# Moving element-wise work between engines in a scan kernel: residuals on VectorE, five products of twelve on GpSimd, and a PSUM bank counted as free later

## The chip, the cores and the metric

The kernel runs on one core of a Trainium2 chip. The core has five engines, each with its own in-order queue of instructions: TensorE (PE, matrix products into PSUM), VectorE (DVE), ScalarE (ACT), GpSimd (POOL) and SyncE (SP), which here only issues DMAs. They wait for one another through semaphores. SBUF is the working memory with 128 partitions; PSUM has eight banks of 128 x 512 float32 numbers, and all eight are used. The metric is the device time of one execution in microseconds, taken as the median of several runs; lower is better.

## The reference

The input is x of shape (4, 96, 64, 64), four images of 96 channels and L = 4096 pixels. Four layers follow one another.

- Layer 0 normalises by groups, multiplies up to 192 channels, applies a 3 x 3 depthwise convolution and SiLU, and then scans the pixels in four orders (rows, columns, and both backwards). The scan is the heart of it: for each of 4 directions, 192 channels and 16 states,

```python
dA = jnp.exp(dt_[..., None] * A[None])
hst = hst * dA + (dt_ * ut)[..., None] * bt[:, :, None, :]
y = jnp.einsum('bkdn,bkn->bkd', hst, ct)
```

 where dt comes out of a softplus, and bt and ct (B and C below) are per state and pixel, shared by the channels. The four directions are summed, normalised over the channels and multiplied down to 96; x is added.
- Layer 1 is an inverted bottleneck: 96 to 576 channels, ReLU, a 3 x 3 depthwise convolution, ReLU, back to 96; x is added.
- Layer 2 normalises each token, mixes the tokens through a 4096-point FFT with a ReLU between transform and inverse, adds the result to x, and then adds a feed-forward network: h = relu(q(q(xn) W1 + b1)), y = q(h W2 + b2), with inputs and weights rounded to an 8-bit and sums to a 16-bit float.
- Layer 3 adds attention without a softmax, which reduces to a product of small matrices per image, plus a bias, and then a feed-forward network like that of layer 2.

## The kernel before

**The scan in units.** A step is one chunk of 512 pixels of one direction of one image: 4 images x 4 directions x 8 chunks = 128 steps. A step has 12 units: 64 channels by 8 states, laid out as 128 partitions by two halves of 512. For each unit,

- GpSimd multiplies the input term with B (`inputs`, line 1206, tile db, 128 x 1024),
- ScalarE forms the two decays exp(A dt) in two PSUM banks of the tag "da" (`decays`, L1216), of which there are four, so two units' worth,
- VectorE runs the two scans (`states`, L1225),
- the states are multiplied with C. There are two kinds of unit. Where the unit's number in its step is in POOL_C, the scans write SBUF (tile hc), GpSimd multiplies both halves in one instruction (`product`, L1244) and copies the final state (L1241). In the others the scans write back into the da banks, VectorE multiplies each half with C into hc (L1229) and ScalarE copies the two final states (L1239). Before, POOL_C holds six of the twelve units,
- TensorE sums the states of two units into the bank "y" (`sums`, L1265), three portions after the first of them, and ScalarE evicts it (L1276).

**The order by portions.** The loop over `slot` in `scans` writes one portion per unit, and the order of the instructions in it is the order of each engine's queue: the DMAs that are due, the decays of the next unit, the product of the last one, db of the unit after the next, the scans of this unit, the sums that are due, and then side work. The side work is everything else: the front of later images (layer 0's convolution and softplus inputs), layers 1 to 3 of earlier images. It is written as generators that yield the engine and the rough cost of the next instruction (`yield ac(0.65)` for ScalarE, `dv` for VectorE, `pe` for TensorE with the number of banks it takes); `advance` takes a step of some stream if the engine has room in this portion (`SHARE`) and if a bank is free. The side work has three banks of the tag "mm", and `held_banks` counts them: `bank` adds one, `free` takes one off. Ahead of each portion's side work the loop also takes `freed[0]` off, which nothing fills before the change.

**Softplus.** `scan_inputs` computes, for each third of the channels, a matmul (L594, L598) into a bank p, three activations on ScalarE (L603, L605, L607), a maximum and sum on VectorE (L609), a product on VectorE (L612), and a copy on ScalarE (L616) that reads p last; then `free()`.

**The feed-forward network.** `feed_forward` normalises (`layer_norm`, L858 to L872), and for each third of the hidden units multiplies (L884), rounds to 16 bits while evicting (L887), adds the bias and applies the ReLU, and rounds to 8 bits. The ReLU is on VectorE (L892) where `alone` is set, and on ScalarE (L895) elsewhere. After the second product (L905) follow the rounding (L908) and the bias (L911) on ScalarE, and the residual: two matmuls with an identity (L914 for the 16-bit result, L915 for x) and a copy on ScalarE (L917). `layer_2` and `layer_3` add their first residual in the same manner, with a matmul of x with the identity (L1030, L1086) into the same bank and an eviction with the bias (L1032, L1088).

**After the scans.** When the loop is over, the list `alone` is filled and the rest is written outside the portions: what is left of layer 1 and all of layers 2 and 3 of the last image, three chunks of 512 pixels at a time. In this part the banks of the scans are taken in turn too.

Of the kernel before, what the change touches and what calls it, by code (L numbers as in the profile page):

```python
# [22 lines left out]
AF = mybir.ActivationFunctionType  # L23
ALU = mybir.AluOpType
# [3 lines left out]
B, C, H, W = 4, 96, 64, 64  # L28
# [13 lines left out]
KORDER = [(0, 1, 3, 2)] * (B - 1) + [(1, 3, 0, 2)]  # L42

SCAN = {"rep_d": 3, "rep_g": 3, "rep_BC": 5, "db": 3, "hc": 5}
POOL_C = (1, 3, 5, 7, 9, 11)
TMP, IN = 10, 5

PC = NI * NJ // 2
# [46 lines left out]
def hybrid_kernel(ctx: ExitStack, tc: tile.TileContext, a: dict):  # L95


    pe, ac, dv = ((lambda us, banks=0, ind=False, e=e: (e, us, banks, ind)) for e in ("pe", "act", "dve"))
    wait = lambda n: ("wait", n, 0, False)
    nc = tc.nc  # L100
    mm = nc.tensor.matmul
    act = nc.scalar.activation
# [11 lines left out]
    alone = []  # L114
# [12 lines left out]

    held_banks, freed = [0], [0]

    def free(n=1):  # L130

        held_banks[0] -= n


    tc.keep_in_program_order(nc.scalar.preload_act_table_set("natural_log_exp_and_others"))
# [5 lines left out]
    def const(name, rows=slice(0, 128)):  # L141
        return cst[rows, CS[name]]

    def col(name, i=0, rows=slice(0, 128)):
        at = COL[name].start + i
        return cols[rows, at : at + 1]
# [29 lines left out]
    def xn_rows(c, rows=128):  # L176
        return xn[:rows, c * RPC : (c + 1) * RPC, :]
# [44 lines left out]
    def chunk(c):  # L222
        return slice(c * CH, (c + 1) * CH)
# [26 lines left out]
    wa2 = small.tile([128, 2, C], F32, name="wa2")  # L250
# [5 lines left out]
    m2 = small.tile([128, C], F32, name="m2")  # L256
    sd, td = (small.tile([128, NT1], F32, name=n) for n in ("sd", "td"))
    t2, ta2 = (small.tile([C, 1], F32, name=n) for n in ("t2", "ta2"))
# [169 lines left out]
    def later(out, t, then=None):  # L428

        to_store.append((out, t, then))  # L430
# [140 lines left out]
    def scan_inputs(b, u, o, c, done):  # L571

        i = b % 3
        if not done.issuperset([c] if o == 0 else range(NCH)):
            while not done.issuperset([c] if o == 0 else range(NCH)):
                yield wait(1)
            yield wait(2)
        ua, ub = u
        yield pe(1.8, 1)
        p = bank()  # L580
        mm(p, lhsT=sel[:, o, 0, :], rhs=view(ua, o, c), start=True, stop=False)
        mm(p, lhsT=sel[:, o, 1, :], rhs=view(ub, o, c), start=False, stop=True)

        yield ac(0.7)
        xd = tmp("xd")
        act(xd, p, AF.Identity, bias=col("one"))
        free()
        for e in (0, 1):
            later(d_bc[o + 2 * e][i][c], xd[64 * e : 64 * e + 2 * NS])
        for part in range(3):  # L590
            yield pe(0.9, 1, part > 0)
            p = bank()
            if part < 2:
                mm(p, lhsT=dtw[:, o + 2 * part, 0:128], rhs=xd, start=True, stop=True)  # L594
                at = [(slice(0, 128), o + 2 * part, slice(0, 128))]
            else:
                for e in (0, 1):
                    mm(p[64 * e : 64 * e + 64], lhsT=dtw[:, o + 2 * e, 128:DI], rhs=xd, start=True, stop=True)  # L598
                at = [(slice(64 * e, 64 * e + 64), o + 2 * e, slice(128, DI)) for e in (0, 1)]

            yield ac(0.65)
            z = tmp("z")
            act(z, p, AF.Abs)  # L603
            yield ac(0.65)
            act(z, z, AF.Exp, scale=-1.0)  # L605
            yield ac(0.65)
            act(z, z, AF.Ln, bias=1.0)  # L607
            yield dv(0.7)
            nc.vector.scalar_tensor_tensor(p, p, 0.0, z, ALU.max, ALU.add)  # L609
            yield dv(0.85)  # L610
            g = tmp("g")
            nc.vector.tensor_mul(split(g), split(p), view(ub if part == 2 else ua, o, c))  # L612
            for rows, k, ch in at:
                later(d_du[k][i][c][ch], g[rows])
            yield ac(0.6)
            nc.scalar.copy(z, p)  # L616
            free()
            for rows, k, ch in at:
                later(d_delta[k][i][c][ch], z[rows])
        traced[b].add((o, c))  # L620
# [254 lines left out]
    def feed_forward(x, weights):  # L875

        wq1, wq2, bq = weights
        xq = tmp("xq", (128, CH), F8)
        yield from layer_norm(x[:C], xq)
        hq = tmp("hq", (128, 3, CH), F8)  # L880
        for m in range(3):
            yield pe(0.5, 1, m > 0)
            p = bank()
            mm(p, lhsT=wq1[:, m * 128 : (m + 1) * 128], rhs=xq, start=True, stop=True)  # L884
            yield ac(0.65)
            acc = tmp("acc16", (128, CH), F16)
            nc.scalar.copy(acc, p)  # L887
            free()
            if alone:

                yield dv(0.75)
                nc.vector.tensor_scalar(acc, acc, bq[:, m : m + 1], 0.0, ALU.add, ALU.max)  # L892
            else:
                yield ac(0.65)
                act(acc, acc, AF.Relu, bias=bq[:, m : m + 1])  # L895
            if alone and m == 1:
                yield dv(0.75)
                nc.vector.tensor_copy(hq[:, m, :], acc, saturate=False)
            else:
                yield ac(0.65)  # L900
                nc.scalar.activation(hq[:, m, :], acc, AF.Copy, saturate=False)  # L901
        yield pe(1.4, 1)
        p = bank()
        for m in range(3):
            mm(p[:C], lhsT=wq2[:, m, :], rhs=hq[:, m, :], start=m == 0, stop=m == 2)  # L905
        yield ac(0.65)
        acc = tmp("acc16", (128, CH), F16)
        nc.scalar.copy(acc[:C], p[:C])  # L908
        free()
        yield ac(0.65)  # L910
        act(acc[:C], acc[:C], AF.Identity, bias=bq[:C, 3:4])  # L911
        yield pe(1.4, 1)
        p = bank()
        mm(p[:C], lhsT=ident16, rhs=acc[:C], start=True, stop=False)  # L914
        mm(p[:C], lhsT=const("ident", slice(0, C))[:, :C], rhs=x[:C], start=False, stop=True)  # L915
        yield ac(0.65)
        nc.scalar.copy(x[:C], p[:C])  # L917
        free()

    def load_x(src, c):  # L920
# [95 lines left out]
    halves_of = {}  # L1016

    def layers_2_and_3(b):
# [3 lines left out]
        def layer_2(c):  # L1022

            x, first = load_x(d_x2[im], c), load_x(d_half[im], c)
            yield wait(3)
            yield pe(2.7, 1)
            p = bank()
            mm(p[:C], lhsT=wa2[:C, 0, :], rhs=first[:C], start=True, stop=False)
            mm(p[:C], lhsT=wa2[:, 1, :], rhs=halves_of[b][:, chunk(c)], start=False, stop=False)
            mm(p[:C], lhsT=const("ident", slice(0, C))[:, :C], rhs=x[:C], start=False, stop=True)  # L1030
            yield ac(0.65)
            act(x[:C], p[:C], AF.Identity, bias=ta2)  # L1032
            free()
            yield from feed_forward(x, ffn[0])
            later(d_x4[im][:C, chunk(c)], x[:C])
            yield from layer_norm(x[:C], xn_rows(c, C), C)
            kv = [tmp("kv"), tmp("kv")]
            for half, t in enumerate(kv):
                yield pe(0.9, 1, half > 0)
                p = bank()  # L1040
                for n in (0, 1):
                    for e in (0, 1):
                        mm(p[64 * e : 64 * e + 64, 2 * C * n : 2 * C * n + 2 * C],
                           lhsT=xn[:, c * RPC + 4 * half + 2 * n + e, :], rhs=wkv, start=True, stop=True)
                yield ac(0.6)
                nc.scalar.copy(t[:, : 4 * C], p[:, : 4 * C])
                free()
            yield pe(0.9, 1)
            pg = bank()
            for n in range(4):  # L1050
                of = kv[n // 2][:, 2 * C * (n % 2) : 2 * C * (n % 2) + 2 * C]
                mm(pg[:C, :C], lhsT=of[:, C:], rhs=of[:, :C], start=n == 0, stop=n == 3)
            yield dv(0.2)
            if "vk" not in small_sums:
                small_sums["vk"] = bp.tile([C, C], F32, name="vk", bufs=1)
                nc.vector.tensor_copy(small_sums["vk"], pg[:C, :C])
            else:
                nc.vector.tensor_add(small_sums["vk"], small_sums["vk"], pg[:C, :C])
            free()
# [20 lines left out]
        def layer_3(c):  # L1080
            x = load_x(d_x4[im], c)
            yield wait(3)
            yield pe(1.8, 1)
            p = bank()
            mm(p[:C], lhsT=m2, rhs=xn_rows(c), start=True, stop=False)
            mm(p[:C], lhsT=const("ident", slice(0, C))[:, :C], rhs=x[:C], start=False, stop=True)  # L1086
            yield ac(0.65)
            act(x[:C], p[:C], AF.Identity, bias=col("bff", rows=slice(0, C)))  # L1088
            free()
            yield from feed_forward(x, ffn[1])  # L1090
            later(a["out"][b][:, chunk(c)], x[:C])

# [480 lines left out]
```

## Time and profile before

| | |
|---|---|
| median of three runs | 6704.47 us (6701.09 to 6705.06) |
| the profiled execution: time, span | 6709.47 us, 6707.7 us |
| VectorE busy in the span | 5391.2 us (80%) |
| GpSimd busy | 5488.7 us (82%) |
| ScalarE busy | 4269.2 us (64%) |
| TensorE busy | 4872.1 us (73%) |
| first scan, last scan | from 79 us to 6208 us |
| products with C on GpSimd (L1244) | 768 x 2361 ns |
| products with C on VectorE (L1229) | 1536 x 692 ns (two to a unit) |

The profile is of one execution. Its page lists groups of instructions by line of the kernel, engine and tiles, with their number, busy time and mean length, and the idle time of the engine just before them with what ended it. A view of the waits sums, for each pair of lines, how long the first waited for the second. A view by windows gives each engine's busy time in a stretch of the span. The chain that ended last is followed back from the last instruction, at each step to what released it. Ends of matmuls are modelled by the profiler. A float32 matmul appears as two instructions.

### The profile page before, as it was taken

The page shows a single profiled execution, that of the slowest core. Times are in us where ns is not written, and L with a number is a line of the kernel's source. Part 1 is how long each engine was busy: PE and PEld are TensorE (multiplying, and loading weights), DVE is VectorE, ACT ScalarE, POOL GpSimd, SP SyncE. Part 2 cuts the span into 40 slices and gives each one's busy share as a digit, 9 for nine tenths or more (in the row PEclk, how much of TensorE's full clock was granted, in tenths as well). Part 3 has the DMA queues.
Part 4 walks back from the last instruction along what each step waited for, and adds up shares of the span by engine and source line. Part 5 has one row for each costly group of instructions (what it writes and reads, how often), then busy time and mean ns, then how long its engine had stood idle before and what let it go on. Part 6 is the DMA issues. An engine that isn't in the chain of part 4 may idle for free. (4 is left out here: it accounts for less than half of the span.)

```text
span 6707.7 us, 84354 instructions
## 1 busy us (share of the span) xinstructions
PE 4872.1 (73%) x27884; PEld 1775.4 (26%) x27884; DVE 5391.2 (80%) x5611; ACT 4269.2 (64%) x8008; POOL 5488.7 (82%) x2983
## 2 busy tenths in 40 slices
PE   7624767656987776775688877777887776859998
PEld 2101212111223521221122254211223521212383
DVE  5979888788989888888899887988988888888021
ACT  5744776654665677877466657866665676756356
POOL 4868778788999999977999988999999899899000
PEclk9756878768998887886799877878998877869998
DMA  5644555566544544455764445465644554554131
GB/s 189 197 150 144 183 189 181 174 218 219 184 148 143 199 158 147 155 186 188 246 214 146 143 160 167 157 219 186 188 147 146 189 161 161 200 180 156 35 94 38
DMA packets 438824, 1121.41 MB, mean 167 GB/s; under 512 B 73002, under 2 KB 74768, under 8 KB 437140
## 3 DMA queue, kind: packets, MB, share of 16 engines
q1 hardware_dynamic: 438388, 1116.02, 50.7%
q8 instruction: 222, 3.64, 0.2%
q14 instruction: 214, 1.75, 0.1%
HBM read 881.28 MB, written 239.01 MB: 167 GB/s over the span
## 5 line engine op out<-in xcount | busy, mean ns | idle before, releaser
L1206 POOL TENSOR_TENSOR db<-rep_g,rep_BC 128x1024 f32<-128x1024 f32 x1536 | 3602.0, 2365 | 194.1 <-DVE ps_da L1225 115.0
L1216 ACT ACTIVATE ps_da<-rep_d,aneg 128x512 f32<-128x512 f32 x3072 | 2053.5, 689 | 499.4 <-DVE hc L1225 381.7
L1225 DVE TENSOR_TENSOR_SCAN ps_da<-ps_da,state,db 128x512 f32<-128x512 f32 x1344 | 1722.9, 1282 | 371.8 <-ACT state L1239 226.7
L1244 POOL TENSOR_TENSOR hc<-hc,rep_BC 128x1024 f32<-128x1024 f32 x768 | 1813.4, 2361 | 131.8 <-DVE hc L1225 64.8
L1225 DVE TENSOR_TENSOR_SCAN hc<-ps_da,state,db 128x512 f32<-128x512 f32 x1344 | 1645.8, 1266 | 173.0 <-ACT ps_da L1216 155.9
L1265 PE MATMUL ps_y<-hc,cst 128*32 128x512 f32 x6144 | 1037.4, 755 | 781.5 <-POOL hc L1244 759.5
L1229 DVE TENSOR_TENSOR hc<-ps_da,rep_BC 128x512 f32<-128x512 f32 x1536 | 1062.3, 692 | 91.3 <-DVE ps_da L1225 1.3
L1265 PEld LDWEIGHTS ps_y<-hc,cst 128*32 128x32 f32 x6144 | 141.7, 119 | 1450.8 <-POOL hc L1244 1096.0
L1241 POOL COPY state<-hc 128x2 f32<-128x2 f32 x672 | 128.4, 191 | 395.3 <-DVE hc L1225 374.1
L1239 ACT COPY state<-ps_da 128x1 f32<-128x1 f32 x1344 | 212.8, 158 | 343.9 <-DVE hc L1229 343.0
L805 PE MATMUL ps_mm<-h,wd 128*32 128x512 f32 x3192 | 365.7, 593 | 7.7 <-ACT r L154 7.0
L543 PE MATMUL ps_mm<-xp,taps 128*128 128x512 f32 x576 | 299.3, 660 | 42.5 <-ACT xp L523 15.7
L1276 ACT COPY yt<-ps_y 128x512 f32<-128x512 f32 x256 | 149.9, 585 | 222.3 <-PE ps_y L1265 212.2
L594 PE MATMUL ps_mm<-xd,dtw 128*128 128x512 f32 x256 | 176.9, 785 | 156.9 <-ACT z L616 131.9
L782 PE MATMUL ps_mm<-wd,w 128*32 128x512 f32 x2128 | 271.4, 624 | 22.9 <-DMA wd<-x 12.8
L1225 DVE TENSOR_TENSOR_SCAN ps_da<-ps_da,db 128x512 f32<-128x512 f32 x192 | 234.6, 1222 | 56.9 <-ACT state L1239 36.0
L1225 DVE TENSOR_TENSOR_SCAN hc<-ps_da,db 128x512 f32<-128x512 f32 x192 | 223.4, 1204 | 17.3 <-ACT ps_da L1216 13.2
L603 ACT ACTIVATE z<-ps_mm 128x512 f32<-128x512 f32 x192 | 114.3, 596 | 189.1 <-PE ps_mm L594 112.4
L609 DVE SCALAR_TENSOR_TENSOR ps_mm<-ps_mm,z 128x512 f32<-128x512 f32 x192 | 131.9, 687 | 84.0 <-ACT z L607 56.4
L864 PE MATMUL ps_mm<-r,cst 128*128 128x512 f32 x210 | 144.9, 778 | 62.7 <-ACT r L154 17.4
L940 PE MATMUL ps_mm<-wa,xp 128*64 128x96 f32 x1728 | 133.3, 317 | 71.0 <-DVE d L944 62.3
L786 ACT ACTIVATE h<-ps_mm 128x512 f32<-128x512 f32 x266 | 153.9, 596 | 44.6 <-PE ps_mm L782 42.5
(418 smaller groups left out, 6879.9 us busy)
## 6 DMA issues: line engine op xcount, KB each, us to landing
rep_BC<-bc SPq DMA_DIRECT2D x512, 512.0 KB
rep_g<-du SPq DMA_DIRECT2D x384, 512.0 KB
rep_d<-delta SPq DMA_DIRECT2D x384, 512.0 KB
y<-yt SPq DMA_DIRECT2D x512, 128.0 KB
du<-g SPq DMA_DIRECT2D x128, 256.0 KB
delta<-z SPq DMA_DIRECT2D x128, 256.0 KB
tab<-in_etab SPq DMA_DIRECT2D x128, 256.0 KB
ypart<-y SPq DMA_DIRECT2D x72, 256.0 KB
```

Of the source, the lines that this page charges most:

```text
L543: mm(p, lhsT=taps[:, t, 0:128], rhs=window(t, c + e), start=t == 0, stop=t == 8)
L594: mm(p, lhsT=dtw[:, o + 2 * part, 0:128], rhs=xd, start=True, stop=True)
L782: mm(p[32 * n : 32 * n + 32], lhsT=w1[:, 32 * g : 32 * g + 32], rhs=xin[:, n : n + 15 : 2, 1 : W + 1], start=True, stop=True)
L786: act(h[:, :, 1 : W + 1], split(p), AF.Relu)
L805: mm(p[32 * n : 32 * n + 32], lhsT=held["wd"][:, groups[i], o, dx, :], rhs=here[i][:, :, dx : dx + W], start=dx == 0, stop=dx == 2)
L1206: nc.gpsimd.tensor_mul(x["db"], x["step"]["g"][x["i"]], both(x["step"]["BC"][x["j"]][:, 0]))
L1216: act(x["da"][e], x["step"]["d"][x["i"]][:, e], AF.Exp, scale=aneg[:, av : av + 1])
L1225: nc.vector.tensor_tensor_scan(x["h"][e][:, order], x["da"][e][:, order], x["db"][:, e, order], start, ALU.mult, ALU.add)
L1229: x["made"] = nc.vector.tensor_mul(x["hc"][:, e], x["h"][e], x["step"]["BC"][x["j"]][:, 1])
L1239: nc.scalar.copy(to[:, e : e + 1], x["h"][e][:, end : end + 1])
L1244: x["made"] = nc.gpsimd.tensor_mul(x["hc"], x["hc"], both(x["step"]["BC"][x["j"]][:, 1]))
L1265: done = mm(y[32 * q : 32 * q + 32], lhsT=const("stack"), rhs=x["hc"][:, e], start=first or (x["pass"] == 0 and x["j"] == 0), stop=last or ...
```

## The change

Four things are edited.

1. `POOL_C` holds five units of twelve instead of six, and other ones: 1, 3, 6, 8 and 10. Seven units of a step are now multiplied on VectorE.
2. In softplus, `free(behind=True)` replaces `free()`: the bank is counted as free only when the side work of the next portion begins, instead of at once.
3. In the tail, where `alone` is set, the residuals are added by VectorE: the first by one `scalar_tensor_tensor` that reads the bank, the bias and x (a new helper `residual`), the second by one `tensor_add` of x and the 16-bit result, so that the matmuls with the identity and the evictions fall away. Inside the scans they stay as they were.
4. The ReLU of the second third of the hidden units (m == 1) is on VectorE inside the scans too.

```diff
-POOL_C = (1, 3, 5, 7, 9, 11)
+POOL_C = (1, 3, 6, 8, 10)
...
-    def free(n=1):
-
-        held_banks[0] -= n
+    def free(behind=False):
+
+        (freed if behind else held_banks)[0] += 1 if behind else -1
...
             nc.scalar.copy(z, p)
-            free()
+            free(behind=True)
...
-            if alone:
+            if alone or m == 1:
...
         act(acc[:C], acc[:C], AF.Identity, bias=bq[:C, 3:4])
+        if alone:
+            yield dv(0.9)
+            nc.vector.tensor_add(x[:C], x[:C], acc[:C])
+            return
         yield pe(1.4, 1)
...
+    def residual(p, x, bias):
+
+        if alone:
+            yield dv(0.75)
+            nc.vector.scalar_tensor_tensor(x[:C], p[:C], bias, x[:C], ALU.add, ALU.add)
+        else:
+            mm(p[:C], lhsT=const("ident", slice(0, C))[:, :C], rhs=x[:C], start=False, stop=True)
+            yield ac(0.65)
+            act(x[:C], p[:C], AF.Identity, bias=bias)
+        free()
...
-            mm(p[:C], lhsT=wa2[:, 1, :], rhs=halves_of[b][:, chunk(c)], start=False, stop=False)
-            mm(p[:C], lhsT=const("ident", slice(0, C))[:, :C], rhs=x[:C], start=False, stop=True)
-            yield ac(0.65)
-            act(x[:C], p[:C], AF.Identity, bias=ta2)
-            free()
+            mm(p[:C], lhsT=wa2[:, 1, :], rhs=halves_of[b][:, chunk(c)], start=False, stop=bool(alone))
+            yield from residual(p, x, ta2)
...
-            mm(p[:C], lhsT=m2, rhs=xn_rows(c), start=True, stop=False)
-            mm(p[:C], lhsT=const("ident", slice(0, C))[:, :C], rhs=x[:C], start=False, stop=True)
-            yield ac(0.65)
-            act(x[:C], p[:C], AF.Identity, bias=col("bff", rows=slice(0, C)))
-            free()
+            mm(p[:C], lhsT=m2, rhs=xn_rows(c), start=True, stop=bool(alone))
+            yield from residual(p, x, col("bff", rows=slice(0, C)))
```

## The prediction, made before the changed kernel was run

> **What bounds the kernel now.** The page's slices show two regimes: the scans (about 79 to 6208 us), in which VectorE and GpSimd are both over 80% busy, and a tail of 500 us in which GpSimd is idle. The page's costliest groups give the prices (engine, operation, tiles, count, busy us, mean ns):
>
> ```profile
> L1244 POOL TENSOR_TENSOR hc<-hc,rep_BC 128x1024 f32<-128x1024 f32 x768 | 1813.4, 2361 | 131.8 <-DVE hc L1225 64.8
> L1229 DVE TENSOR_TENSOR hc<-ps_da,rep_BC 128x512 f32<-128x512 f32 x1536 | 1062.3, 692 | 91.3 <-DVE ps_da L1225 1.3
> ```
>
> One product on GpSimd is 2.36 us, the same on VectorE 2 x 0.69. Next I cut the span by stages (busy us of PE, PE's loads, VectorE, ScalarE, GpSimd; clock, DMA share, GB/s): a front, a convolution, layers 2 and 3 inside the scans, the tail.
>
> ```profile
> 599.00:1046.00 447.00, 294.49 (x884) 82.05 (x884) 377.83 (x401) 298.73 (x551) 348.45 (x189) 0.78 0.55 178
> 1630.00:2103.00 473.00, 392.94 (x2275) 109.83 (x2272) 430.49 (x437) 299.96 (x587) 466.10 (x256) 0.93 0.52 169
> 2382.00:2781.00 399.00, 262.65 (x937) 75.58 (x934) 352.07 (x360) 320.75 (x622) 385.42 (x212) 0.78 0.45 149
> 6208.00:6708.00 500.00, 439.23 (x4022) 251.01 (x4014) 77.42 (x155) 263.83 (x413) 2.37 (x1) 0.94 0.18 56
> ```
>
> The convolution holds 131 of the db products, 11 steps of 12 units: 43.0 us a step, GpSimd 99% busy. Layers 2 and 3: 9 steps of 44.3 us, GpSimd 97%, VectorE 88%. The front: 8 steps of 55.9 us, GpSimd 78%, VectorE 85%. Who keeps VectorE waiting, in the convolution and then in the layers (total us, times, longest):
>
> ```profile
> DVE ps_da L1225 <- POOL db L1206: 29.1, 42, 1.1
> DVE ps_da L1225 <- ACT state L1239: 5.0, 4, 2.5
> ```
> ```profile
> DVE ps_da L1225 <- ACT state L1239: 18.2, 19, 2.4
> DVE hc L1225 <- ACT ps_da L1216: 8.2, 11, 1.5
> ```
>
> In the convolution GpSimd alone ends VectorE's waits; in the layers it is ScalarE, itself late behind side matmuls. In the whole kernel's waits softplus shows: TensorE waits for the copy that frees a bank, then ScalarE for that matmul.
>
> ```profile
> PE ps_mm L594 <- ACT z L616: 131.9, 59, 6.2
> ACT z L603 <- PE ps_mm L594: 112.4, 70, 5.1
> ```
>
> In the tail the chain that ended last runs through the residuals (start us, us, what):
>
> ```profile
> 6535.66 0.63 ACT acc L911
> 6536.33 0.59 PE ps_da L914
> 6536.91 1.71 PE ps_da L915 x2
> 6539.05 1.71 PE ps_da L915 x2
> 6541.18 0.94 PE ps_mm L915 x2
> 6542.12 0.86 PE ps_mm L858 x2
> ```
>
> **What the Trainium skill says.** "SBUF — State Buffer", section "Who interferes with whom": VectorE and GpSimd share a port pair under an exclusive lock; a VectorE instruction with two SBUF inputs, or in a two-port mode, is shut out for the whole of a GpSimd instruction that started first. "VectorE: DVE Perf Modes", section "The perf-mode tier table": a 16-bit tensor_scalar from SBUF to SBUF takes the 4x mode, which uses both ports. The trace agrees on the lock. Timeline, two engines:
>
> ```profile
> 4372.04 2.48 DVE L1065 TENSOR_TENSOR vk<-vk,cst 96x96 f32<-96x96 f32 x1
> 4372.07 4.67 POOL L1206 TENSOR_TENSOR db<-rep_g,rep_BC 128x1024 f32<-128x1024 f32 x2
> ```
>
> L1065 takes 0.25 us in the tail and 2.48 here, until the GpSimd product has ended. Groups by shape:
>
> ```profile
> L737 DVE SCALAR_TENSOR_TENSOR xc<-ps_mm,wout_bias,xc 96x512 f32<-96x512 f32 x31 | 23.2, 747 | 1.1
> L952 DVE TENSOR_TENSOR d<-d,rib 1x96 f32<-1x96 f32 x16 | 19.8, 1235 | 0.4
> L892 DVE TENSOR_SCALAR acc<-acc,bq 128x512 f16<-128x512 f16 x48 | 15.6, 348 | 13.3 <-ACT acc L887 13.3
> ```
>
> L952 takes 0.35 us alone (its median in the tail), but 1.24 over all 16, four of them in the tail: (16 x 1.24 - 4 x 0.35) / 12 = 1.53 beside GpSimd, so 1.18 us of lock. Every L892 so far is in the tail, so no row shows the lock for it; a copy with a single SBUF input, L393, took 1.79 us for 192 elements beside GpSimd. L1229 and the scans have one SBUF input and keep their length beside GpSimd.
>
> **The change part by part.** The durations are from the profiled execution (6709.47 us, span 6707.7); the median of the runs is 5.0 us below it, so differences are carried over to 6704.5.
>
> *Residuals in the tail.* Of 16 chunks each loses L1030 or L1086 (two passes of 0.43 = 0.86 us on TensorE), L914 and L915 (2.1 us by the starts above), an eviction of 0.68 and a copy of 0.58 on ScalarE; it gains an operation like L737 (0.75) and an addition that I price at 0.75 too. The chunks go in groups of 3, 3, 2 a layer. On the chain: 16 x 0.86 = 13.8 for the first residual; from L914 to the next group of instructions 5.8, 6.5 and 4.4 us in layer 2, and 3.4, 3.4 and 5.1 in layer 3: 28.6. In return six additions stand open, 4.5; one group still waits for its x (DMA, 3.75 us in the chain), 2 of the gain lost; and TensorE, idle during the additions, runs cold afterwards (L915 above takes 1.71 us where a warm pair takes 0.86), up to 0.86 x 6 = 5. Net -31; ends -20 and -40. GpSimd is idle here, so nothing waits for the lock. Stores and loads keep their number; only what they follow moves from ScalarE to VectorE.
>
> *Five of twelve.* In each of 128 steps GpSimd loses 2.36 + 0.19 us; VectorE gains 1.38, ScalarE two state copies of 0.16. In the convolutions and the last image (40 steps, 1729 us, 43.2 a step) GpSimd falls to 43.0 - 2.55 = 40.5 and VectorE rises to 430.5/11 + 1.38 = 40.5: level. Two queues that wait for each other don't both run full; I take 42.2, so -40. Ends 0 and -92 (all the way to about 40.9). In layers 2 and 3 (30 steps, 1376 us) VectorE gains 42 us, in the fronts (29 steps, 1581 us) 40, in the spectral stages (18 steps) 25, in turn and weights (11 steps) 15.
>
> *The second relu of the feed-forward network* (line 889's condition) comes with it: in the scans 48 activations of 0.72 leave ScalarE, and 48 L892 come to VectorE at 0.35 + 1.18 of lock = 1.53, 73 us in all, in the layers. The relu's price is bounded by 48 x 0.35 = 17 (GpSimd idle each time) and 48 x (0.35 + 2.36) = 130. Behind it on VectorE stands the next unit's scan, and behind that ScalarE's decays, which need the bank, and GpSimd's product. So the layers get 115 us more VectorE work against 1376 - 1168 = 208 us of idle. I let a quarter show: +30; ends -10 and +115.
>
> *The bank.* Taken off the count a portion later, it moves the next matmul out of the portion whose copy it waited for. The waits it aims at: TensorE 132 for L594 and 106 for L598, ScalarE 112 and 75 behind them. What VectorE feels of that is part of the waits for ScalarE. Cost: a stream starts later; in the built order the second front ends some four units later, with no deadline near. In the fronts I set +25 of the 40 us of products against -30 of waits: -5; ends -60 and +50. The spectral stages, where VectorE's own long runs alternate with slack, 0 (+-15); turn -8, weights +4 (+-15).
>
> Sum: -31 - 40 + 30 - 5 + 0 - 8 + 4 = -50; 6704.5 - 50 gives **6655**.
>
> **The rivals.** *VectorE pays for everything (slower).* Outside the 40 calm steps its new work is 42 + 73 + 40 + 25 + 15 = 195 us. If its waits for ScalarE stay as they are, as the layers' table suggests (GpSimd is not the releaser there), all of it shows: 6704.5 + 195 - 71 = 6829. From 71/195 = 36% on, the tail and the calm steps are used up; at half it is 6731. Against it: in the layers GpSimd is 97% busy, so some of ScalarE's lateness is GpSimd's through TensorE, whose longest waits are for GpSimd's products. *The waits go with their cause (much faster).* VectorE absorbs the products in its idle time, the calm steps reach 41, the softplus waits vanish: -35 - 80 + 0 - 40 - 10 = -165, 6540; at two thirds 6595. For it: VectorE is idle 12 to 15% in those stages. Against: its queue is in order, and the lock stays. *A wash:* calm steps gain nothing because both queues stand at 40.5 of work and wait for each other, and half the layers' idle fills: -31 + 0 + 35 - 5 = about 0, 6704. That a part does not happen is excluded: the built order has 32 new VectorE operations in the tail, 256 more products and 48 more relus.
>
> **How the numbers follow.** Forecast 0.52 (6610 to 6690 by itself), much faster 0.18, wash 0.11, slower 0.19. A measurement of this kernel tells about 0.2% (13 us) from no change: faster 0.70, same 0.11, slower 0.19. For 8 in 10 the range leaves out the outer ends of both strong rivals: 6580 to 6738.
>
> **What would show it.** Right: a tail of about 470 us without L915; convolution steps near 42 us with VectorE over 95% and GpSimd under 97%; L892 inside the scans at a mean near 1.5 us; L594's waits for L616 mostly gone. Wrong: convolution steps still at 43; layers over 46.5 us a step with VectorE's waits for ScalarE undiminished; fronts over 56 a step because the waits moved on.

## The result, and the profile after

| | before | after |
|---|---|---|
| median of the runs, side by side | 6702.78 us | 6596.74 us (6584.09 to 6604.82) |
| ratio to before | | 0.9838, 95% interval 0.9826 to 0.9850 |
| profiled execution: time, span | 6709.47, 6707.7 us | 6604.82, 6603.1 us |
| last scan ends at | 6208 us | 6130 us |
| stretch after the last scan | 499.8 us | 473.2 us |

The kernel is 106 us faster, about twice what was forecast. Lines after L911 carry new numbers: the scan L1225 is now L1234, the decays L1216 are L1225, the products L1229 and L1244 are L1238 and L1253, db is L1215, the state copies L1239 and L1241 are L1248 and L1250, the sums L1274.

The costliest groups of the page show that the edit of `POOL_C` is what it says: 128 products less on GpSimd, 256 halves more on VectorE, at the same length of one.

```profile
L1253 POOL TENSOR_TENSOR hc<-hc,rep_BC 128x1024 f32<-128x1024 f32 x640 | 1512.0, 2363 | 116.0 <-DVE hc L1234 59.4
L1238 DVE TENSOR_TENSOR hc<-ps_da,rep_BC 128x512 f32<-128x512 f32 x1792 | 1239.3, 692 | 109.8 <-PE ps_y L1274 1.5
```

The same four stretches of the span, by windows (busy us of PE, PE's loads, VectorE, ScalarE and GpSimd; clock, DMA share, GB/s): a front, a convolution, layers 2 and 3, the stretch after the scans.

```profile
617.00:1026.00 409.00, 277.41 (x868) 77.53 (x872) 382.34 (x411) 300.12 (x564) 324.76 (x172) 0.79 0.58 189
1567.00:2026.00 459.00, 400.28 (x2296) 111.73 (x2288) 440.47 (x457) 301.34 (x607) 440.99 (x236) 0.93 0.54 176
2326.00:2734.00 408.00, 270.35 (x942) 80.19 (x942) 380.30 (x393) 314.94 (x620) 362.79 (x193) 0.77 0.45 146
6130.00:6603.00 473.00, 404.31 (x3938) 236.43 (x3930) 99.97 (x188) 244.10 (x381) 0.00 (x0) 0.94 0.19 59
```

The convolution went from 473 to 459 us, with VectorE and GpSimd now level at 96%. The layers grew from 399 to 408, the tail shrank from 500 to 473. The surprise is the first line. The same eight steps of the front took 447 us and now take 409, although VectorE is busy 4.5 us longer in them: its time without work fell from 69 to 27 us.

The scan's own work in a step is the same in both kernels, 12 units. Side work can move to another step, and a sum by steps then moves with it; here little did: of the 192 copies of softplus (L616), 186 start in the 29 front steps before and 183 after. Cut at the start of each step's first scan, the steps of a kind sum to (us, profiled executions):

| steps | before | after | difference | forecast |
|---|---|---|---|---|
| fronts (29) | 1580.7 | 1489.1 | -91.6 | -5 |
| calm: convolutions and last image (40) | 1728.6 | 1682.0 | -46.6 | -40 |
| layers 2 and 3 (30) | 1375.0 | 1411.2 | +36.2 | +30 |
| spectral (18) | 866.6 | 881.2 | +14.6 | 0 |
| turn (8) | 373.7 | 366.9 | -6.8 | -8 |
| weights (3) | 204.2 | 220.3 | +16.1 | +4 |
| after the last scan | 499.8 | 473.2 | -26.6 | -31 |

The executions differ by 105 us where 50 were forecast. The fronts alone gained 87 us more than forecast; the other rows together gained 32 less. What VectorE waited for in those eight steps, before and after (total us, times, longest):

```profile
DVE ps_da L1225 <- ACT state L1239: 30.0, 11, 7.7
DVE hc L1225 <- ACT ps_da L1216: 12.6, 7, 6.0
DVE ps_mm L609 <- ACT z L607: 6.1, 8, 2.1
DVE ps_mm L609 <- ACT state L1239: 5.6, 5, 1.6
...
DVE ps_da L1225 <- ACT ps_da L1216: 3.2, 2, 1.7
```
```profile
DVE ps_da L1234 <- ACT state L1248: 9.4, 7, 2.2
DVE g L612 <- DMA du<-g: 4.7, 1, 4.7
DVE hc L1234 <- ACT ps_da L1225: 3.4, 2, 2.5
DVE ps_mm L609 <- ACT z L607: 0.5, 1, 0.5
DVE hc L1234 <- ACT state L1248: 0.2, 1, 0.2
```

Its waits for ScalarE went from 57.5 to 13.5 us. In the waits of the whole kernel, the two links ahead of that, which stood at 131.9 and 112.4 us before, and TensorE's wait at the other matmul of softplus, before and after:

```profile
PE ps_mm L594 <- ACT z L616: 56.2, 30, 4.3
ACT z L603 <- PE ps_mm L594: 40.3, 32, 6.2
```
```profile
PE ps_mm L598 <- ACT z L616: 106.1, 42, 5.6
```
```profile
PE ps_mm L598 <- ACT z L616: 60.9, 29, 7.2
```

The waits of VectorE in the convolution and in the layers, the other two views shown of before:

```profile
DVE ps_da L1234 <- ACT state L1248: 5.5, 5, 1.8
DVE ps_da L1234 <- ACT ps_da L1225: 2.5, 3, 1.4
```
```profile
DVE ps_da L1234 <- ACT state L1248: 7.8, 8, 2.7
DVE ps_da L1234 <- ACT ps_da L1225: 4.7, 3, 2.0
```

In the convolution, VectorE's wait for GpSimd's db (29.1 us before) is gone. In the layers its waits for ScalarE were halved too, and yet the layers take longer: there VectorE is busy 28 us more. In the tail, the chain that ended last now goes from the bias through one addition to the next layer's norm, with no L915 in it:

```profile
6455.46 0.63 ACT acc L911
6456.12 0.70 DVE xc L914
...
6456.86 3.78 PE ps_da L858 x4
```

From the end of L911 to the first L858 there were 5.8 us before (6536.29 to 6542.12); here there are 0.8. Some of it comes back at once: four L858 take 3.78 us, where the pair shown before took 0.86; the granted clock in these 3.8 us is 0.50.

### The profile page after: what moved, and what is told of

The parts are those of the page before. It is cut to its first block, busy times and chain, and to the rows that moved or that the text cites. A ratio compares the mean times of both kernels' runs of the same rounds, so it can differ in the third digit from the quotient of the medians.

```text
span 6603.1 us, 84466 instructions
## 1 busy us (share of the span) xinstructions
PE 4803.7 (73%) x27804; PEld 1767.2 (27%) x27804; DVE 5616.6 (85%) x5947; ACT 4265.1 (65%) x8152; POOL 5183.5 (79%) x2743
## 5 line engine op out<-in xcount | busy, mean ns | idle before, releaser
L1215 POOL TENSOR_TENSOR db<-rep_g,rep_BC 128x1024 f32<-128x1024 f32 x1536 | 3601.2, 2365 | 474.3 <-DVE ps_da L1234 357.7
L1225 ACT ACTIVATE ps_da<-rep_d,aneg 128x512 f32<-128x512 f32 x3072 | 2067.3, 690 | 557.2 <-DVE hc L1234 423.1
L1234 DVE TENSOR_TENSOR_SCAN ps_da<-ps_da,state,db 128x512 f32<-128x512 f32 x1568 | 2005.6, 1279 | 209.8 <-ACT state L1248 162.0
L1253 POOL TENSOR_TENSOR hc<-hc,rep_BC 128x1024 f32<-128x1024 f32 x640 | 1512.0, 2363 | 116.0 <-DVE hc L1234 59.4
L1274 PE MATMUL ps_y<-hc,cst 128*32 128x512 f32 x6144 | 1024.8, 745 | 660.9 <-POOL hc L1253 413.4
L1234 DVE TENSOR_TENSOR_SCAN hc<-ps_da,state,db 128x512 f32<-128x512 f32 x1120 | 1371.3, 1266 | 82.2 <-ACT ps_da L1225 54.8
L1238 DVE TENSOR_TENSOR hc<-ps_da,rep_BC 128x512 f32<-128x512 f32 x1792 | 1239.3, 692 | 109.8 <-PE ps_y L1274 1.5
L1248 ACT COPY state<-ps_da 128x1 f32<-128x1 f32 x1568 | 247.8, 158 | 525.4 <-DVE hc L1238 521.5
L1274 PEld LDWEIGHTS ps_y<-hc,cst 128*32 128x32 f32 x6144 | 145.9, 118 | 1298.1 <-POOL hc L1253 641.4
L1250 POOL COPY state<-hc 128x2 f32<-128x2 f32 x560 | 106.8, 191 | 353.1 <-DVE hc L1234 337.1
L805 PE MATMUL ps_mm<-h,wd 128*32 128x512 f32 x3192 | 366.9, 595 | 8.7 <-ACT r L154 8.7
L543 PE MATMUL ps_mm<-xp,taps 128*128 128x512 f32 x576 | 299.5, 663 | 52.2 <-ACT ua L545 21.5
L1234 DVE TENSOR_TENSOR_SCAN ps_da<-ps_da,db 128x512 f32<-128x512 f32 x224 | 273.0, 1219 | 41.0 <-ACT state L1248 27.8
L594 PE MATMUL ps_mm<-xd,dtw 128*128 128x512 f32 x256 | 171.0, 760 | 101.3 <-ACT z L616 56.2
L1234 DVE TENSOR_TENSOR_SCAN hc<-ps_da,db 128x512 f32<-128x512 f32 x160 | 186.0, 1203 | 3.0 <-ACT ps_da L1225 2.9
L786 ACT ACTIVATE h<-ps_mm 128x512 f32<-128x512 f32 x266 | 152.4, 596 | 48.2 <-PE ps_mm L782 46.6
L543 PEld LDWEIGHTS ps_mm<-xp,taps 128*128 128x128 f32 x576 | 116.7, 210 | 230.4 <-issue 163.2
L805 PEld LDWEIGHTS ps_mm<-h,wd 128*32 128x32 f32 x3192 | 105.5, 109 | 251.9 <-issue 210.1
```

The lines of the kernel that those rows point to most:

```text
L543: mm(p, lhsT=taps[:, t, 0:128], rhs=window(t, c + e), start=t == 0, stop=t == 8)
L786: act(h[:, :, 1 : W + 1], split(p), AF.Relu)
L805: mm(p[32 * n : 32 * n + 32], lhsT=held["wd"][:, groups[i], o, dx, :], rhs=here[i][:, :, dx : dx + W], start=dx == 0, stop=dx == 2)
L1215: nc.gpsimd.tensor_mul(x["db"], x["step"]["g"][x["i"]], both(x["step"]["BC"][x["j"]][:, 0]))
L1225: act(x["da"][e], x["step"]["d"][x["i"]][:, e], AF.Exp, scale=aneg[:, av : av + 1])
L1234: nc.vector.tensor_tensor_scan(x["h"][e][:, order], x["da"][e][:, order], x["db"][:, e, order], start, ALU.mult, ALU.add)
```

## The experiments

The first four runs take the change apart; the later ones set the reasons for the fronts' gain against each other. Four were thought of. *Wait*: a matmul that needs the bank whose copy (L616) still stands in ScalarE's queue blocks TensorE; ScalarE then waits for that matmul, and the decays and state copies behind it reach VectorE late. *Pace*: holding a bank a portion longer only spreads the softplus parts over more portions. *Products*: the fronts gained from five of twelve. *Relu*: what moved in the layers shifted everything after it. Each run stands beside runs of the kernel before on the same chip (medians 6701.2, 6703.1 and 6706.0 us in the three groups).

**The bank alone**, in the kernel before:

```diff
-            free()
+            free(behind=True)
```


> The kernel before with softplus's bank counted as free a portion later, and nothing else. Theory 1 (the bank is what made the fronts 92 us shorter: the matmul behind the copy no longer holds TensorE and, through it, ScalarE and VectorE): the 29 front steps fall from 1581 us to about 1500, the other stages stay within 15 us, 60 to 100 us off the kernel before. Theory 2 (the fronts gained from the products, because TensorE's sums and everything behind them wait less for GpSimd): the fronts stay above 1560 and the time within 20 us of before. Theory 3 (both are needed: each alone leaves the other's wait): 20 to 50 us.

Measured: 6630.07 us, ratio 0.9897 (0.9882 to 0.9911), 71 us less. The fronts took 1464.7 us, 116.0 less than before. The same eight steps by windows, and what VectorE waited for in them:

```profile
609.30:1008.30 399.00, 275.26 (x864) 75.60 (x864) 371.59 (x394) 297.01 (x548) 343.42 (x186) 0.81 0.59 193
```
```profile
DVE ps_da L1225 <- ACT state L1239: 7.0, 4, 2.2
DVE hc L1225 <- ACT ps_da L1216: 4.2, 2, 2.5
...
DVE ps_mm L609 <- ACT z L607: 1.2, 2, 0.8
...
DVE ps_mm L609 <- ACT state L1239: 0.4, 1, 0.4
```

12.8 us of waits for ScalarE instead of 57.5, seven VectorE instructions fewer fall into the stretch, 6 us of its work. TensorE's waits for the copy, in the whole kernel:

```profile
PE ps_mm L594 <- ACT z L616: 62.4, 27, 4.9
PE ps_mm L598 <- ACT z L616: 61.0, 22, 5.1
```

The bank does it, without any product moved. The layers lost 27.5 us and the weights 15.6 in this run, where nothing in them was edited.

**The bank at once**, in the changed kernel (the edit above undone):

```diff
-            free(behind=True)
+            free()
```


> The changed kernel with the bank counted as free at once, as before. Theory 1: the fronts go back to 1580 us or more (VectorE has 40 us more to do there), the time to 6680 to 6710. Theory 2: fronts stay near 1490, the time near 6600. Theory 3: fronts 1520 to 1560, time about 6640.

Measured: 6698.78 us, ratio 0.9999 (0.9990 to 1.0007). Without the bank the rest of the change is worth nothing. The fronts are back at 1592.5 us, 103 above the changed kernel.

**Five of twelve alone**, in the kernel before:

```diff
-POOL_C = (1, 3, 5, 7, 9, 11)
+POOL_C = (1, 3, 6, 8, 10)
```


> The kernel before with POOL_C = (1, 3, 6, 8, 10) and nothing else. If the calm stages' gain is the products': the 40 steps of convolution and last image fall from 1729 us to about 1685. Under theory 1 the fronts rise by 10 to 40 us and the time is 10 to 50 us below before; under theory 2 the fronts fall by over 60 and the time by over 100.

Measured: 6709.82 us, ratio 1.0011 (1.0005 to 1.0018). The calm steps gained 50.3 us; the fronts lost 12.0, the layers 20.3, spectral 10.8, weights 11.6. The products gain where GpSimd bounds and cost elsewhere, and the sum is a small loss, where a gain of 10 to 50 us was expected under the first theory.

**The relu back on ScalarE**, in the changed kernel:

```diff
-            if alone or m == 1:
+            if alone:
```


> The changed kernel with the second third's ReLU on ScalarE inside the scans again. If the 36 us that the layers lost come from the 48 VectorE instructions that wait for GpSimd's port (1.18 us each in the profile of after, 57 us in sum): layers 1411 us to about 1375, the time 25 to 45 us below the changed kernel, some 6560. Rival: ScalarE's queue needs the 0.72 us each more than VectorE does, and the layers' loss is the products': the time is the same within 10 us or longer.

Measured: 6604.88 us, ratio to before 0.9854 (0.9838 to 0.9871), which overlaps that of the changed kernel; the layers took 1412.9 us against 1411.2. Neither sum moved. Within the layers two moves cancel: with the relu back on ScalarE the first 20 of the 30 steps took 25 us less (919.3 against 944.2) and the last ten 27 us more (493.6 against 467.0). The order of the side work differs too (133 of the rounding copies L887 start in the layers, against 139), so what the relu costs by itself isn't separated from what it shifts. (The 1.18 us in the expectation is the whole length of an L892; the part beyond its 0.35 us is 0.83.)

**Paced, with the bank at once**, in the kernel before:

```diff
-            yield dv(0.7)
+            yield dv(0.9)
             nc.vector.scalar_tensor_tensor(p, p, 0.0, z, ALU.max, ALU.add)
-            yield dv(0.85)
+            yield dv(1.05)
```


> The kernel before, its bank still free at once, with softplus's two VectorE portions booked at 0.9 and 1.05 us instead of 0.7 and 0.85, so that the planner spreads the softplus parts over more portions (at most 10 a step, and the stage's last parts a step later). Theory 'wait' (the 71 us of the bank edit alone came from matmuls L594/L598 that stood at the head of TensorE's queue until ScalarE had copied z out of the same bank): the waits of L594 and L598 for L616, 238 us before, stay above 170 us, and the time stays within 6680 to 6725. Theory 'pace' (holding a bank a portion longer only spread the parts): 6610 to 6660, without any wait taken away on purpose.

Measured: 6716.23 us, ratio 1.0019 (1.0012 to 1.0025). Of this run's waits, of the whole kernel:

```profile
PE ps_mm L594 <- ACT z L616: 115.9, 50, 5.2
PE ps_mm L598 <- ACT z L616: 108.8, 37, 6.4
```

The waits stayed at 224.7 us of 238.0, and the time with them. By steps the run looks different: the fronts took 72 us less (1509.0) and the calm steps 53 more (1781.8). Here side work did move, as the number of softplus parts in the fronts shows. VectorE in the 29 front steps (us; a part is a copy L616, of 192):

| | fronts | VectorE busy | without work | waits for ScalarE | softplus parts |
|---|---|---|---|---|---|
| before | 1581 | 1360 | 221 | 183 | 186 |
| bank alone | 1465 | 1347 | 118 | 78 | 183 |
| paced | 1509 | 1315 | 194 | 153 | 156 |
| two portions behind (below) | 1407 | 1322 | 85 | 53 | 124 |

Pacing hands 30 parts on to later steps, and 45 of its 72 us are work that left the fronts. The bank alone hands on three, and 103 of its 116 us are time in which VectorE had nothing to do. So spreading the parts, further than the bank edit does, doesn't bring what the bank brought. This run also shows what lateness costs: the scans ended 12 us earlier (6196), and the stretch behind them took 519 us, since the last image's side work was not as far.

**Two portions behind**, in the changed kernel:

```diff
-    held_banks, freed = [0], [0]
+    held_banks, freed = [0], [0, 0]
...
-        (freed if behind else held_banks)[0] += 1 if behind else -1
+        if behind:
+            freed[-1] += 1
+        else:
+            held_banks[0] -= 1
...
-            held_banks[0] -= freed[0]
-            freed[0] = 0
+            held_banks[0] -= freed.pop(0)
+            freed.append(0)
```


> The changed kernel, with softplus's bank counted as free two portions behind its copy instead of one. Theory 'wait': the 117 us that L594 and L598 still wait for L616 fall below 50, the fronts lose a further 10 to 50 us, and the time is 6550 to 6590. Rival 'held too long' (three banks only: a part that holds one for a portion more leaves the other streams without a bank, and the parts run past the front stages): fronts no faster, stages after them longer, 6600 to 6660.

Measured: 6623.12 us, ratio 0.9879 (0.9864 to 0.9893), 26 us more than the changed kernel. Its waits (the lines are three further on: L597 and L601 are L594 and L598, L619 is L616), and the stretch after its last scan, in two windows:

```profile
PE ps_mm L597 <- ACT z L619: 17.3, 16, 3.3
PE ps_mm L601 <- ACT z L619: 13.5, 10, 2.7
```
```profile
6078.00:6160.00 82.00, 77.75 (x436) 23.93 (x436) 6.84 (x12) 27.64 (x44) 0.00 (x0) 0.96 0.23 58
6160.00:6627.00 467.00, 399.96 (x3994) 236.88 (x3984) 98.04 (x185) 245.08 (x382) 0.00 (x0) 0.94 0.18 53
```

Both theories had a part. The waits fell from 117 to 31 us and the scans ended 52 us earlier, at 6078. But the longer hold pushed the side work back (62 softplus parts fewer in the fronts than before, so that their 1407 us aren't all gain), and 549 us were left after the scans instead of 473: in the first 82 of them TensorE is busy for 78. One portion is a balance between the wait and the lateness, and the wait alone doesn't set the time.

**The tail alone**, in the kernel before. The residuals of the changed kernel (`residual` and L914) and nothing else; the relu, the bank and the products are as before.

> The kernel before with the VectorE residuals of the last image's layers alone: six products of twelve, the bank free at once, the relu of the second block on ScalarE during the scans. Nothing before the last scan differs. If the residuals are worth what the stretch after the last scan says (499.8 us before, 473.2 in the changed kernel): 6670 to 6682. If part of those 27 us comes from how late the last image's side work stood when the scans ended, and not from the residuals: 6684 to 6700.

Measured: 6678.74 us, ratio 0.9957 (0.9941 to 0.9972), 27 us less, with 470 us after the last scan. Everything ahead of that scan is the same code as before, and in its profiled execution the scans still took 14 us less: so much a sum over all steps moves by itself. Most of it fell on the fronts, spectral and turn, 3 to 4 us each.

**Six of twelve throughout**, in the changed kernel (`POOL_C` as before):

> The changed kernel with six products of twelve in every step: bank, residuals and relu without the five of twelve. If the parts add (bank -71, residuals -27, the five of twelve about nothing in all): 6595 to 6612, the same as the changed kernel. If the five of twelve needed the bank to pay (the kernel before had other waits in its way), or the bank needed them: more than 6620.

Measured: 6589.87 us, ratio 0.9828 (0.9812 to 0.9844): not told apart from the changed kernel, and a little under what adding the parts gave. Against it, the five of twelve gave 50 us to the calm steps (1731.7 to 1682.0) and took 29 from the fronts, 23 from the layers and 13 from spectral. The parts alone (bank -71, tail -27, products +9) sum to -90, the change gave -106; those 16 us, little more than the 14 above, aren't explained.

**Five where it pays, six elsewhere**, from the changed kernel:

```diff
-POOL_C = (1, 3, 6, 8, 10)
+CALM = set(range(28, 39)) | set(range(66, 76)) | set(range(93, 104)) | set(range(120, 128))
+POOL_C = lambda n: (1, 3, 6, 8, 10) if n in CALM else (1, 3, 5, 7, 9, 11)
...
-                                      "pool": u in POOL_C})
+                                      "pool": u in POOL_C(number)})
```


> The changed kernel, where GpSimd has five products of twelve in the 40 calm steps (convolutions and the last image) only, and six in all the others. If the five-of-twelve edit pays in each stage as its runs alone and against the bank's run say (calm -50, fronts +12 to +24, spectral +11 to +20, layers +9 to +20, weights and turn about 0): calm steps stay at 42 us, fronts fall to about 50.5 us a step, and the time is 6535 to 6570. If the stages only hand time to one another (what one saves the next waits for): 6585 to 6610.

Measured: 6539.83 us, ratio 0.9750 (0.9734 to 0.9767), 57 us under the changed kernel. Calm 1690.9, fronts 1464.3, spectral 861.6, layers 1389.1. The fronts and the layers have what they had with six throughout, and the calm steps keep 38 us of their 47.

**Seven in the fronts**, added to that: `(1, 3, 5, 6, 8, 10, 11)` for steps 0 to 5, 9 to 23 and 54 to 61.

> As the run with six elsewhere, but seven of twelve in the 29 front steps, where VectorE was busy 93% and GpSimd 79% of the second half of the front. A product moved to GpSimd takes 2 x 0.69 = 1.38 us from VectorE and gives 2.36 us to GpSimd, so both would stand near 45 us of a 50 us step. If VectorE's time bounds the fronts: a further 10 to 40 us less than with six, 6505 to 6550. If the chain through GpSimd's product to the sums (L1274) and the wait for ScalarE bound them: equal to or up to 30 us above the run with six.

Measured: 6529.09 us, ratio 0.9738 (0.9723 to 0.9752); the intervals of this run and the last overlap. In the eight steps VectorE and GpSimd are level now, but neither is full:

```profile
607.30:1006.70 399.40, 278.55 (x864) 76.85 (x864) 360.72 (x378) 295.03 (x534) 359.19 (x200) 0.80 0.59 192
```

Both are busy 90%, and the stretch takes the 399 us that it took with six and the bank. Over all 29 front steps VectorE has 40 us less to do than in the last run (1307 against 1347), and they took 12.5 us less (1451.8 against 1464.3), within what a sum moves by itself. VectorE's work is no longer the main bound of the fronts.

**The fronts' other banks behind too** (the copies out of the input convolution and into xd: `free(behind=True)` in three more places), once in the changed kernel and once with the products of the last run:

> The changed kernel with the banks of ScalarE's other copies in the fronts (the input convolution's three, and xd) counted as free a portion behind too. In the changed kernel TensorE's matmuls L543, L552, L581 and L594 wait for those copies for some 40 us in all, against 238 us for softplus's copy before. If what pays is the wait that is taken away: 6575 to 6598. If a bank held longer costs more there than it saves, since the front then ends later and work is handed to the stretch after the last scan, as with two portions: 6602 to 6640.

> Seven products of twelve in the fronts, five in the calm steps, six elsewhere (6529 us), with the input convolution's banks and xd's free a portion behind as well. In that kernel the matmuls' waits for xd and ua were some 30 us. If the waits count: 6505 to 6530. If the longer hold costs more: 6532 to 6570.

Measured: 6570.67 us, ratio 0.9798 (0.9783 to 0.9812), and 6515.27 us, ratio 0.9716 (0.9702 to 0.9731). The last is the fastest kernel of the study, 81 us under the changed one. Why the first gains 26 us, more than was expected of it, stays open: side work moves here too (165 softplus parts in the fronts), so that the fronts' 45 us less and the calm steps' 52 more than in the changed kernel don't tell; the waits of the fronts' matmuls for ua and xd fell from 94 to 75 us, but those for z rose from 148 to 168, and their sum stayed (sums over L543, L552, L581, L594, L598).

## Why the prediction was right in kind and half in size

VectorE's account over the scans, from the windows and the sums of its waits by what ended them (us; what is left over has no releaser in the profile):

| | scans | VectorE busy | waits for ScalarE | waits for GpSimd |
|---|---|---|---|---|
| before | 6129 | 5299 | 521 | 144 |
| bank alone | 6048 | 5304 | 384 | 181 |
| five alone | 6132 | 5459 | 479 | 17 |
| after | 6051 | 5502 | 338 | 18 |

From before to after VectorE took 203 us more work and lost 184 of waits for ScalarE and 127 of waits for GpSimd: -108, of which 78 show; the rest is waits for DMAs and TensorE (+15) and time with no releaser in the profile. Five alone traded 159 us of work for 127 of waits for GpSimd and 42 for ScalarE, an even exchange; the bank alone took away 137 of waits for ScalarE at no work.

**The bank in the fronts: the step that failed.** The term was "+25 of the 40 us of products against -30 of waits: -5". The +25 was right: 24.4 between the bank's run and the changed kernel, 29 against six throughout. The -30 measured -116 alone and -103 inside the change. It even passed the outer end that the prediction gave its fronts, -60. The chain of causes was named as it turned out; what VectorE feels of it was called a part of its waits for ScalarE, and then set at -30 without reading that part. The view was there. In the eight steps shown those waits are 57.5 us, and the bank alone took 45 of them; counted over all 29 front steps they are 183 us before and 78 with the bank alone, 105 less. TensorE's own waits for L616 point the same way: they fell by 115 us (238.0 to 123.4) in the run with the bank alone, about as much as the fronts' 116. The sign that the prediction gave, L594's waits mostly gone, came only in part: 56 of 132 us stayed.

**The tail.** -31 forecast, -26.6 in the stretch and -27 in its own run. L915 is gone, and the slow L858 are the cost that the working allowed for.

**Five of twelve in the calm steps.** -40 forecast at 42.2 us a step, -46.6 at 42.05. The level at which both engines stand is 96%, over 95 for VectorE and under 97 for GpSimd as listed. One reading was off: the working took GpSimd's work for the whole step, 43.0 us, where its busy time was 466.1 / 11 = 42.4, so it should have fallen to 39.8 and not to 40.5. In the run it stands at 40.1 us a step and VectorE at 40.0; the estimate of 42.2 didn't depend on it.

**The layers.** +30 forecast, +36.2 measured, but for other reasons, so the nearness is luck. The relu, 73 of the 115 us of work behind that figure, costs nothing that the sum of the layers could tell. The products cost 23 of their 42 (against six throughout), where a quarter was let through. The rest is not settled: the bank alone, which edits nothing in the layers, made them 27.5 us longer, 23 of it in the last ten steps. Within six throughout, where bank and relu are both in, it is 13.

**Relu under the lock.** 1.53 us forecast for L892 inside the scans, 1178 ns measured, so 57 us instead of 73.

**Weights, spectral, turn.** +4, 0 and -8 forecast; +16, +15 and -7 measured. In the spectral steps 13 of the 15 are the products (against six throughout), for which nothing was put. The weights lose as much with the bank alone (15.6) and nearly as much with five alone (11.6); why stays open.

**The rivals.** "VectorE pays for everything" is refuted as a whole, since the time fell. For the products outside the calm steps it was half right: of their 122 us of new work about 65 show against six throughout (fronts 29, layers 23, spectral 13), and the bank paid for it. "The waits go with their cause" had the mechanism, but put 40 us of it into the fronts, 80 into the calm steps and none on the layers; its 6540 is on the other side of the result for that reason. That its figure at two thirds, 6595, is 2 us from the measured 6597 is luck: the stages don't add up that way. "A wash" is what the change is without the bank.

## What to carry to other kernels

Read the waits of the bounding engine stage by stage, and price an edit that removes their cause from what they hold there, not at a share chosen for caution: the bounding engine's 183 us of waits in the fronts were there to read, and halving two waits further up the queue, of 132 and 106 us in all, took away 105 of them. A buffer whose last reader stands in another engine's in-order queue should not be given to the next matmul in the same breath; one portion later was worth 71 us, two pushed other work past the end and gave 26 back. Where side work can move, check first whether a stage that got shorter still holds the same work. A balance between two engines is a setting for a stage, not for a kernel: five of twelve throughout was worth nothing, and in 40 chosen steps 50 us.

## What the runs showed of the hardware

L892, a 16-bit tensor_scalar from SBUF to SBUF, takes much longer in the scans than in the tail. Groups by shape, first of the scans, then of the stretch after them:

```profile
L892 DVE TENSOR_SCALAR acc<-acc,bq 128x512 f16<-128x512 f16 x48 | 56.6, 1178 | 10.0 <-ACT acc L887 10.0
```
```profile
L892 DVE TENSOR_SCALAR acc<-acc,bq 128x512 f16<-128x512 f16 x48 | 15.7, 349 | 12.7 <-ACT acc L887 12.6
L914 DVE TENSOR_TENSOR xc<-xc,acc 96x512 f32<-96x512 f32 x16 | 10.3, 688 | 16.2 <-ACT acc L911 16.2
```

L914, the new addition, comes to 688 ns with GpSimd idle, near the 0.75 us it was priced at. For L892, in the 48 instances inside the scans the length isn't a spread around a mean: 40 end between 147 and 162 ns after the end of a GpSimd product that was running, and the other 8 take 321 to 355 ns. Timeline, two engines:

```profile
5344.48 4.71 POOL L1215 TENSOR_TENSOR db<-rep_g,rep_BC 128x1024 f32<-128x1024 f32 x2
5345.44 1.54 DVE L892 TENSOR_SCALAR acc<-acc,bq 128x512 f16<-128x512 f16 x1
```

The two products of the first row end at about 5346.83 and 5349.19, and L892 at 5346.98. This is the exclusion that the Trainium skill describes ("SBUF — State Buffer", "Who interferes with whom"), for a form of which the kernel before had no example beside GpSimd. Two details were not expected. The mean wait is 0.83 us and not the 1.18 taken over from L952, because L892 often begins late in a product or outside one. And the two instances that began 29 and 48 ns before a product's end did not slip through: they were held for the whole of the next one, 2.50 and 2.53 us. L1065 in the prediction's timeline is a third: it began 0.06 us before the end of an L1244 product and, by the recorded starts, 0.03 us before the L1206 product that it was held for. So which of the two "started first", as the prediction has it, can't be read off recorded starts this close.
